# A pre-LN graph layer on one core: SyncE's row fetches on a semaphore per batch, sixteen batches of them, and four edits at the start and the end

## The chip, the cores and the metric

The kernel runs on one core of a Trainium2 chip. The metric is the device time of one execution in microseconds (us), the median of several runs. A core has five engines that run their own instruction streams in order: PE (TensorE, matmuls), DVE (VectorE), ACT (ScalarE), POOL (GpSimd) and SP (SyncE, which issues transfers). SP, ACT and POOL start DMA transfers; engines wait for each other and for transfers through semaphores.

## What is computed

12500 nodes have 160 features each, 64 scalars and 32 vectors of three. 400000 edges, sorted by destination, carry 16 numbers (inputs of a small network that gives 192 weights an edge) and 4 numbers (one scalar and one vector). Cut to what matters:

```python
h  = relu(layernorm(x))                          # per node
y0 = h[:, :64] @ W_l1_0 * attr / 8               # scalars
y1 = einsum('nuc,uv->nvc', h1, W_l1_1) * attr    # vectors
w  = silu(e16 @ W1) @ W2                         # 192 weights per edge
ys0, ys1 = y0[src], y1[src]                      # gather by source
mid = products of w, ys and the edge's 4 numbers # 96 scalars, 96 vectors
z  = zeros.at[dst].add(mid)                      # scatter by destination
o  = z @ W_l2 * attr
out = x + C_S * (h @ W_sc) * attr + C_X * o
```

## The kernel before

**Node stage.** Nodes come in 98 tiles of 128, two tiles to a step. A step does the layernorm and the ReLU on VectorE, turns the rows and maps them by `W_l1` on PE (`map_rows`, L499 in the trace), scales them on ACT and stores them from SP to `y_d` in DRAM. Meanwhile POOL fetches raw rows of `x` for 18 "x batches" (`x_fetch`, L392: 72 indirect DMAs of 128 rows) into `xr`, a buffer of 18 slots. Each fetch issued in step q waits for the maps of step q - 6.

**Main loop.** An edge tile is 128 edges; a batch is four tiles; there are 782 batches, the last with one tile. For each batch the loop does:

- `weigh`: the small network's second matmul on PE (L689) and a copy by ACT (L568);
- `products`: on VectorE a one-hot of the edge's place in its window (`own`, L704), its product with the edge's 4 numbers (`sel`, L706), and the gathered rows times the weights (`pr`, L573 and L577);
- `sums`: on PE the matmul of `sel` and `pr` (L720), which adds the edges of a window into PSUM; a finished window is transposed by VectorE (L726, L727);
- once a group of windows is full: `linear` (L733 on PE, a copy on ACT L735, `place` on VectorE L737), `add` (L745) and `accumulate` into `acc` (L756);
- `extras`: the small network's first layer (L668, L673) for batches to come, a step of the skip path (`skip_load` of `xs` on SP L766, `skip_center` on VectorE L773, turns on PE L780, maps, `skip_add`) and of the x batches, which are mapped inside the loop and need no row of `y_d`.

The order of instructions on every engine is the order of the program text; it is written out by hand. `products(b + 1)` comes ahead of `sums(b)`, and small actions that are put off (`waiting`, two at most) run right behind the products.

**Where the rows come from.** The products need 512 rows of `y_d`, one per edge. Most batches get them by four indirect DMAs on POOL (`gather`, L615), issued six batches ahead and kept in step with the sums. The x batches need none. For some other batches the rows are fetched singly, by a job: a job is (s, b, m), it starts at batch s, fetches 512 rows of 640 bytes spread over m batches, and its rows are used by batch b = s + m + 7. SP has the jobs s = RS, RS + RB, ...; with RB = 58 and RS = 30 these are 12. ACT has 10, with AB = 66 and AS = 102. `row_index` loads the node numbers of eight jobs at a time and `row_place` makes byte places of them; then

- SP does a chunk of 32 rows (`RN`) each m/16 batches: a load of 32 places into registers (L626, the trace's TENSOR_LOAD), then 32 times a register move and a DMA of one row (L638);
- ACT does eight rows (`RU`) in every batch of its job, with a register load for each 16.

The rows of a job go to a slot of `xr` that is free by then. SP's rows are tracked by the framework: it puts each DMA on one of eight semaphores in rotation ("lanes"), a DMA waits until the one before it on its lane has landed, and VectorE's products wait for the lanes. ACT's rows have a semaphore of their own for the batch (`came[b]`); each adds 16, no lane is used, and VectorE waits once for 16 x 512 (`all_rows`).

SP's queue in the loop holds, beside the chunks, the loads of edge data (`xe` L407, 4-number features and indices L415 to L419), a store of `drel` (L433) and the 160 KB loads of `xs` (L766).

**The end.** In the last three batches nothing is put off any more; behind the loop the last two groups get their `linear`, `add` and `accumulate`. Eight tiles of `out` are stored by SP and ACT (L355) after that; a branch for edges outside their windows is not taken with this data. The program's end (L1159) drains every engine.

Of the kernel before, what the change touches and what calls it, by code (L numbers as in the profile page):

```python
# [12 lines left out]
U8 = mybir.dt.uint8  # L13
# [9 lines left out]
D = M0 + 3 * M1  # L23
# [20 lines left out]
LATE = 8  # L44
XB = 18
SK = 9
RB = 58
RS = 30
AB = 66
AS = 102  # L50
RN = 32
AN = 16
RU = 8
# [7 lines left out]
def kernel(  # L61
# [328 lines left out]
    def x_fetch(f, after):  # L390
        u, k = divmod(f, GT)
        fetch = nc.gpsimd.indirect_dma_start(  # L392
            out=xr[:, u, slot(k), :], out_offset=None, in_=x,
            in_offset=bass.IndirectOffsetOnAxis(ap=xi[:, u, k:k + 1], axis=0))
        if after is not None:
            tc.add_manual_dep(fetch.ins, after,
                              mybir.DependencyInfo(mybir.DependencyClass.Sync, mybir.DependencyReason.DATA),
                              reason="rows keep step with the maps")
# [40 lines left out]
    with (  # L439
# [90 lines left out]
        for q in range(len(steps) + 7):  # L530
            if q <= last and steps[q][2] == 0 and more:
                load_x(*more.pop(0))
            for f in range(XB * GT * q // (last + 6), min(XB * GT * (q + 1) // (last + 6), XB * GT)):
                x_fetch(f, mapped.get(q - 6))
            if q == 8:
                e4_load(0)
            for load in loads[2 * q - 24:2 * q - 22] if q >= 12 else []:
                load()
            if q == 24:
                for b in range(min(EARLY, NB)):  # L540
                    features(b)
            if q == 16:
                rows_of_windows()
                lowest(0)
            if q == 18:
                pt = nd_ph.tile([MW, P], F32, name="ph")[:windows_in(0), :]
                turn_low(0, pt)
                most(0, pt)
            if q == 22:
                spread(0, nd_ph.tile([P, MW], F32, name="ph")[:, :windows_in(0)])  # L550
            for stage, lag in ((scales, 3), (leave, 7), (out_of_psum, 4), (roots, 2), (turn_rows, 3), (map_rows, 5),
                               (moments, 0), (center, 1)):
                if 0 <= q - lag <= last:
                    stage(q - lag)
            if q == 2:
                node_weights()
            if q == last + 3:
                nc.vector.tensor_scalar(nm, mv[:, :, 0], -1.0, None, ALU.mult)
                x_split()
                edge_weights()  # L560
                relate(rp, 0)
# [18 lines left out]
    with (  # L580
# [43 lines left out]
        def row_places(j, n, m, engine):  # L624
            q, o = divmod(n, P // RP * GT)
            _, places = nc.values_load_multi_w_load_instructions(  # L626
                ri[RP * j + q:RP * j + q + 1, o:o + m], engines=[engine], min_val=0, max_val=(N - 1) * D * 4,
                skip_runtime_bounds_check_because="places of nodes, as the indices of the other fetches")
            return places

        def row_fetch(j, n, eng, places):
            b = jobs[j][1]
            if n == 0:
                rows[b] = xr[:, slot_of[j], :, :]
            fetches = []
            for m, v in enumerate(places):
                e, k = divmod(n + m, GT)
                fetches.append(eng.dma_start(rows[b].bitcast(U8)[e:e + 1, k, :], y_b[ds(v, D * 4)].unsqueeze(0)))  # L638
            return fetches

        def row_fetch_by_sp(j, n):
            row_fetch(j, RN * n, nc.sync, row_places(j, RN * n, RN, mybir.EngineType.SP))

        def row_fetch_by_act(j, n):
            o = RU * n % AN
            if n == 0:
                came[jobs[j][1]] = tc.alloc_semaphore(f"rows_{j}"), f"rows_{j}"
            sem, group = came[jobs[j][1]]
            for fetch in row_fetch(j, RU * n, nc.scalar, places_of[j][o:o + RU]):
                fetch.then_inc(sem, 16)  # L650
                tc.no_tile_sem_insts.add(fetch.ins.name)
                tc.add_to_no_dep_group(group, fetch.ins)

        def act_places(j, n):
            if RU * n % AN == 0:
                places_of[j] = row_places(j, RU * n, AN, mybir.EngineType.Activation)

        def all_rows(b):
            if b in came:
# [37 lines left out]
        def products(b):  # L697

            n, wt, yg = slots_of(b), wts.pop(b), rows.pop(b)
            all_rows(b)  # L700
            own = selp.tile([P, GT, WN], F32, name="own")
            sel = sels[b] = selp.tile([P, GT, 4, WN], F32, name="sel")[:, :n, :, :]
            pr = prs[b] = prod.tile([P, GT, PC], F32, name="pr")
            nc.vector.tensor_tensor(own[:, :n, :], iota[:, 0:WN].unsqueeze(1).to_broadcast([P, n, WN]),  # L704
                                    wt[:, :n, NW + 4:NW + 5].to_broadcast([P, n, WN]), ALU.is_equal)
            nc.vector.tensor_tensor(sel, own[:, :n, :].unsqueeze(2).to_broadcast([P, n, 4, WN]),  # L706
                                    wt[:, :n, NW:NW + 4].unsqueeze(3).to_broadcast([P, n, 4, WN]), ALU.mult)
            multiply(pr, wt, yg, n)
# [20 lines left out]
        def linear(g):  # L729
            m, za = WN * windows_of(g), zT.pop(g)  # L730
            po = p_x.tile([P, D], F32, name="px")
            for k in range(ZK):
                nc.tensor.matmul(po[:m, :], za[:, k, :m], wo[:, k, :], start=k == 0, stop=k == ZK - 1)  # L733
            os = post.tile([P, D], F32, name="os")
            nc.scalar.activation(os[:m, :], po[:m, :], AF.Copy)  # L735
            place = post.tile([P, 2, P], F32, name="place")
            nc.vector.tensor_scalar(place.rearrange("p h n -> p (h n)"), iota, at[:, g:g + 1], None, ALU.is_equal)  # L737
            o_sb[g] = os, place
# [208 lines left out]
            weigh(1)  # L947
        products(0)
        early = [x for x in groups if x[0] < LOW]
        assert early[-1][0] + early[-1][1] == LOW and first_of[GE] + K + len(early) <= NB  # L950
        for b in range(NB):
            g = group_of[b]
            k = b - first_of[g]
            if b + EARLY < NB:
                features(b + EARLY)
            q, r = divmod(b, KB)
            if b % 8 == 0 and RG * b // 8 < len(jobs):
                row_index(b // 8)
            if r == 0:
                e4_load(q + 1)  # L960
            if r == KB - 4:
                e4_join(q + 1)
            u, v = divmod(b, PER)
            su, sv = skip_of(b)
            if b + 2 < NB:
                weigh(b + 2)
            if units and units[0][0] <= b:
                act_places(*units[0][1:])
            if b + 1 < NB:
                products(b + 1)  # L970
            while waiting and b + K < NB:
                waiting.pop(0)()
            if b % 8 == 2 and RG * (b // 8) < len(jobs):
                row_place(b // 8)
            if v == SB and u < XB:
                x_scale(u)
            if v == 11 and u + 1 < XB:
                hot(u + 1)
            if r == KB - 15 and q + 1 < NQ:
                lowest(q + 1)  # L980
            if r == KB - 8 and q + 1 < NQ:
                relate(rp, q + 1)
                if q + 2 == NQ:
                    most_far()
            if early and b > first_of[GE] + K - 1:
                store(*early.pop(0), nc.sync)
            sums(b)
            for m, part in ((b + AHEAD - 1, slice(2, GT)), (b + AHEAD, slice(0, 2))):
                if AHEAD <= m < NB and m not in xs_of and m not in rows_of:
                    gather(m, part)  # L990
            while chunks and chunks[0][0] <= b:
                row_fetch_by_sp(*chunks.pop(0)[1:])
            while waiting and b + K >= NB:
                waiting.pop(0)()
            extras(b)
            if units and units[0][0] <= b:
                row_fetch_by_act(*units.pop(0)[1:])
        while waiting:
            waiting.pop(0)()
        assert max(b for b in range(NB) if 0 <= skip_of(b)[0] < NU) <= first_of[GE] + K and NQ > 1  # L1000
        for h in ([NG - 2] if NG > 1 else []) + [NG - 1]:
            for k, stage in enumerate((linear, add, accumulate)):
                if h == NG - 1 or min(k, 1) > NB - 1 - first_of[NG - 1]:
                    stage(h)
        order.close()


# [155 lines left out]
```

## Time and profile before

| | before |
|---|---|
| runs | 4938.69, 4900.01, 4903.42 us |
| median | 4903.42 us |
| profiled execution, its own time | 4914.76 us |
| its span | 4912.9 us |
| granted TensorE clock, mean | 0.883 |
| row fetches by SP (L638) | 6144 |
| row fetches by ACT (L638) | 5120 |
| gathers by POOL (L615) | 2965 |
| fetches of x's rows by POOL (L392) | 72 |

The profile is of one execution; its times count from the start of its span. In a row of a group stand line, engine, operation, output<-inputs and count, then busy time and the mean duration in ns, then the idle time ahead of it and what ended most of it. In a row of a source line stand queue, operation, count, the shortest, median and longest duration in ns, and the first and last start in us. In a row of the waits: who, for what, us in total, times, the longest. In a row of a timeline: start, duration, engine, line, operation and how many in a row were put together. In a row of windows: the window, its length, VectorE's busy time there with the count of instructions, granted clock, share of the DMA engines that were busy, GB/s. An engine's name with a q at its end is its sequencer, which issues DMAs.

### The profile page before, as it was taken

Reading aid. Unit: us, or ns where it says so; the run is one execution under the profiler, and the core shown is the slowest. Engines: PE = TensorE matmul, PEld = TensorE weight load, DVE = VectorE, ACT = ScalarE, POOL = GpSimd, SP = SyncE. Lnnn points to the kernel's source line nnn. Section 1 sums busy time; section 2 is a strip of 40 time slices with the busy share of each in tenths; the row PEclk is TensorE's granted clock in tenths of the full one; section 3 lists DMA queues with packets and bytes.
Section 4 is the critical chain, followed back from the end, with each engine's and each line's share of the span. In section 5 each row is a group of like instructions: output and inputs, shape, how many; then the busy total and the mean of one; then the engine's idle time right before and its main releaser. Section 6 shows DMA issues by size and latency. Waiting matters only on the chain. (4 is left out here: it accounts for less than half of the span.)

```text
span 4912.9 us, 76368 instructions
## 1 busy us (share of the span) xinstructions
PE 3930.2 (80%) x17274; PEld 2517.5 (51%) x17274; DVE 2747.3 (56%) x6901; ACT 609.6 (12%) x1863; POOL 2878.2 (59%) x3045
## 2 busy tenths in 40 slices
PE   7778887767778686887777787888887888888888
PEld 7444544444445454554454555555554555555555
DVE  5455555544555454555455565566565666666666
ACT  5011011101101010111011111111111111111110
POOL 6666665646656565555556556566556555565654
PEclk8889898878989898988899898899898888999889
DMA  7222222222222222222222222222222222222223
GB/s 194 67 69 64 70 66 64 60 55 65 65 57 65 58 66 59 64 61 61 56 64 65 63 57 66 61 67 64 64 60 64 61 65 61 65 63 62 65 61 109
DMA packets 272510, 330.52 MB, mean 67 GB/s; under 512 B 84288, under 2 KB 223456, under 8 KB 272048
## 3 DMA queue, kind: packets, MB, share of 16 engines
q0 software_dynamic: 145776, 248.99, 20.5%
q1 hardware_dynamic: 115408, 73.03, 5.3%
q10 hardware_dynamic: 10864, 3.57, 0.4%
q8 instruction: 140, 2.29, 0.2%
q14 instruction: 322, 2.64, 0.2%
HBM read 307.72 MB, written 17.61 MB: 66 GB/s over the span
## 5 line engine op out<-in xcount | busy, mean ns | idle before, releaser
L615 POOL DMA_INDIRECT yg<-y_d,src_q x2965 | 2808.5, 947 | 1962.4 <-issue 702.5
L720 PE MATMUL pz<-pr,sel 128*128 128x320 f32 x6250 | 2122.9, 486 | 51.4 <-issue 23.2
L720 PEld LDWEIGHTS pz<-pr,sel 128*128 128x128 f32 x6250 | 1244.4, 210 | 726.2 <-issue 384.3
L689 PE MATMUL pw<-w,hT 64*128 64x192 f32 x6250 | 825.4, 387 | 331.4 <-DVE pr L577 168.3
L689 PEld LDWEIGHTS pw<-w,hT 64*128 64x128 f32 x6250 | 567.4, 210 | 632.0 <-issue 512.1
L726 DVE STREAM_TRANSPOSE za<-pz 128x160 f32<-128x160 f32 x598 | 206.2, 345 | 1050.5 <-PE pz L720 443.5
L577 DVE TENSOR_TENSOR pr<-pw,yg 128x384 f32<-128x384 f32 x1484 | 749.4, 546 | 0.0
L706 DVE TENSOR_TENSOR sel<-own,pw 128x512 f32<-128x512 f32 x782 | 536.8, 686 | 28.3 <-DVE own L704 1.4
L573 DVE TENSOR_TENSOR pr<-pw,yg 128x512 f32<-128x512 f32 x742 | 506.2, 682 | 9.3 <-DMA yg<-y_d,src_q 9.3
L704 DVE TENSOR_TENSOR own<-iota,pw 128x128 f32<-128x128 f32 x782 | 204.8, 262 | 511.2 <-issue 265.3
L668 PE MATMUL px<-xe,w 32*128 32x512 f32 x782 | 442.1, 648 | 40.5 <-issue 15.9
L568 ACT ACTIVATE pw<-ev 128x20 f32<-128x20 f32 x782 | 149.2, 191 | 2472.6 <-DMA xr<-y_d 526.1
L673 ACT ACTIVATE hT<-px 128x512 f32<-128x512 f32 x391 | 233.2, 597 | 972.4 <-remote 220.5
L733 PEld LDWEIGHTS px<-wo,za 128*128 128x128 f32 x1500 | 227.4, 203 | 153.2 <-issue 77.6
L733 PE MATMUL px<-wo,za 128*128 128x160 f32 x1500 | 261.5, 325 | 53.0 <-issue 11.9
L668 PEld LDWEIGHTS px<-xe,w 32*128 32x128 f32 x782 | 115.6, 185 | 220.0 <-issue 180.4
L745 PE MATMUL px<-os,place 128*128 128x160 f32 x600 | 127.7, 340 | 116.6 <-ACT os L735 94.6
L727 DVE STREAM_TRANSPOSE za<-pz 32x160 f32<-32x160 f32 x598 | 202.0, 338 | 21.6 <-DVE za L726 1.2
L780 PE MATMUL px<-ident,sh 128*128 128x128 f32 x98 | 31.7, 341 | 219.7 <-DVE sh L773 180.3
L745 PEld LDWEIGHTS px<-os,place 128*128 128x128 f32 x600 | 100.0, 209 | 163.2 <-ACT os L735 114.5
L773 DVE TENSOR_SCALAR sh<-xs,mv 128x160 f32<-128x160 f32 x98 | 26.5, 309 | 251.9 <-DMA xs<-in_x 251.9
L780 PEld LDWEIGHTS px<-ident,sh 128*128 128x128 f32 x98 | 15.9, 163 | 241.0 <-issue 176.4
(129 smaller groups left out, 1623.7 us busy)
## 6 DMA issues: line engine op xcount, KB each, us to landing
xr<-y_d SPq DMA_DIRECT2D x6144, 0.6 KB
xr<-y_d ACTq DMA_DIRECT2D x5120, 0.6 KB
yg<-y_d,src_q POOLq DMA_INDIRECT x2965
xe<-in_e SPq DMA_DIRECT2D x196, 128.0 KB
xs<-in_x SPq DMA_DIRECT2D x48, 160.0 KB
acc<-in_x SPq DMA_DIRECT2D x11, 640.0 KB
y_d<-ys SPq DMA_DIRECT2D x11, 640.0 KB
out<-acc SPq DMA_DIRECT2D x11, 640.0 KB
```

The lines of the kernel that those rows point to most:

```text
L573: nc.vector.tensor_mul(pr[:, :n, :].rearrange("p t (x u) -> p t x u", x=2)[:, :, :, 0:M0], wt[:, :n, 0:NW].rearrange("p t (x u) -> p t x u ...
L577: nc.vector.tensor_mul(pr[:, :n, D * x + M0:D * (x + 1)].rearrange("p t (c u) -> p t c u", c=3), wt[:, :n, 96 * x + M0:96 * (x + 1)].unsqu ...
L615: fetch = nc.gpsimd.indirect_dma_start(out=yg[:, slot(t), :], out_offset=None, in_=y_d, in_offset=bass.IndirectOffsetOnAxis(ap=ev4[t // BL ...
L668: nc.tensor.matmul(ph, w1[r, :], xe[r, :], start=True, stop=True)
L673: nc.scalar.activation(hT, ph, AF.Silu, scale=1.0 / math.sqrt(FC_IN))
L689: nc.tensor.matmul(pw[:, k, 0:NW], hT[r, o:o + P], w2[r, :], start=True, stop=True)
L704: nc.vector.tensor_tensor(own[:, :n, :], iota[:, 0:WN].unsqueeze(1).to_broadcast([P, n, WN]), wt[:, :n, NW + 4:NW + 5].to_broadcast([P, n, ...
L706: nc.vector.tensor_tensor(sel, own[:, :n, :].unsqueeze(2).to_broadcast([P, n, 4, WN]), wt[:, :n, NW:NW + 4].unsqueeze(3).to_broadcast([P, ...
L720: mm = nc.tensor.matmul(pz[:, 0:PC], sel[:, slot(t), :, :], pr[:, slot(t), :], start=o == 0, stop=last)
L726: nc.vector.transpose(zT[g][:, :, at_w], pz[:, D:PC].rearrange("p (k u) -> p k u", k=ZK))
L733: nc.tensor.matmul(po[:m, :], za[:, k, :m], wo[:, k, :], start=k == 0, stop=k == ZK - 1)
L745: nc.tensor.matmul(ps[:, h, :], place[:m, h, :], os[:m, :], start=True, stop=True)
```

## The change

1. SP's row fetches get a semaphore for each batch, as ACT's have: `row_fetch` does for both what `row_fetch_by_act` did, so VectorE waits once for an SP batch too.
2. The jobs change: SP 16 of 44 batches from batch 26 (for 12 of 58 from 30), ACT 10 of 65 from 108 (for 10 of 66 from 102).
3. `x_fetch` in step q waits for the maps of step q - 9 and not q - 6.
4. In the last three batches (`ends`): in batch 779 `products(780)` comes behind `sums(779)`, and what waits goes ahead; in batch 780 `linear` of the last group but one comes ahead of `sums(780)`, its `add` behind it. No `extras` are called there, and behind the loop only the last group is left.
5. POOL drains at batch 775, behind its last gather.

```diff
--- before.py
+++ after.py
@@ -44,10 +44,10 @@
 LATE = 8
 XB = 18
 SK = 9
-RB = 58
-RS = 30
-AB = 66
-AS = 102
+RB = 44
+RS = 26
+AB = 65
+AS = 108
 RN = 32
 AN = 16
 RU = 8
@@ -531,7 +531,7 @@
             if q <= last and steps[q][2] == 0 and more:
                 load_x(*more.pop(0))
             for f in range(XB * GT * q // (last + 6), min(XB * GT * (q + 1) // (last + 6), XB * GT)):
-                x_fetch(f, mapped.get(q - 6))
+                x_fetch(f, mapped.get(q - 9))
             if q == 8:
                 e4_load(0)
             for load in loads[2 * q - 24:2 * q - 22] if q >= 12 else []:
@@ -632,28 +632,25 @@
             b = jobs[j][1]
             if n == 0:
                 rows[b] = xr[:, slot_of[j], :, :]
-            fetches = []
+                came[b] = tc.alloc_semaphore(f"rows_{j}"), f"rows_{j}"
+            sem, group = came[b]
             for m, v in enumerate(places):
                 e, k = divmod(n + m, GT)
-                fetches.append(eng.dma_start(rows[b].bitcast(U8)[e:e + 1, k, :], y_b[ds(v, D * 4)].unsqueeze(0)))
-            return fetches
-
-        def row_fetch_by_sp(j, n):
-            row_fetch(j, RN * n, nc.sync, row_places(j, RN * n, RN, mybir.EngineType.SP))
-
-        def row_fetch_by_act(j, n):
-            o = RU * n % AN
-            if n == 0:
-                came[jobs[j][1]] = tc.alloc_semaphore(f"rows_{j}"), f"rows_{j}"
-            sem, group = came[jobs[j][1]]
-            for fetch in row_fetch(j, RU * n, nc.scalar, places_of[j][o:o + RU]):
+                fetch = eng.dma_start(rows[b].bitcast(U8)[e:e + 1, k, :], y_b[ds(v, D * 4)].unsqueeze(0))
                 fetch.then_inc(sem, 16)
                 tc.no_tile_sem_insts.add(fetch.ins.name)
                 tc.add_to_no_dep_group(group, fetch.ins)
 
+        def row_fetch_by_sp(j, n):
+            row_fetch(j, RN * n, nc.sync, row_places(j, RN * n, RN, mybir.EngineType.SP))
+
         def act_places(j, n):
             if RU * n % AN == 0:
                 places_of[j] = row_places(j, RU * n, AN, mybir.EngineType.Activation)
+
+        def row_fetch_by_act(j, n):
+            o = RU * n % AN
+            row_fetch(j, RU * n, nc.scalar, places_of[j][o:o + RU])
 
         def all_rows(b):
             if b in came:
@@ -947,6 +944,7 @@
             weigh(1)
         products(0)
         early = [x for x in groups if x[0] < LOW]
+        assert NG > 1 and NB - first_of[NG - 1] == 2 and NB > K
         assert early[-1][0] + early[-1][1] == LOW and first_of[GE] + K + len(early) <= NB
         for b in range(NB):
             g = group_of[b]
@@ -966,10 +964,13 @@
                 weigh(b + 2)
             if units and units[0][0] <= b:
                 act_places(*units[0][1:])
-            if b + 1 < NB:
+            ends = b + K >= NB
+            if b + 1 < NB and not (ends and b + 2 < NB):
                 products(b + 1)
-            while waiting and b + K < NB:
+            while waiting and (not ends or b + 2 < NB):
                 waiting.pop(0)()
+            if b + 2 == NB:
+                linear(NG - 2)
             if b % 8 == 2 and RG * (b // 8) < len(jobs):
                 row_place(b // 8)
             if v == SB and u < XB:
@@ -990,18 +991,24 @@
                     gather(m, part)
             while chunks and chunks[0][0] <= b:
                 row_fetch_by_sp(*chunks.pop(0)[1:])
-            while waiting and b + K >= NB:
+            if ends and b + 2 < NB:
+                products(b + 1)
+            if b + 2 == NB:
+                add(NG - 2)
+                waiting.append(lambda: accumulate(NG - 2))
+            while waiting and ends:
                 waiting.pop(0)()
-            extras(b)
+            if not ends:
+                extras(b)
+            if b + 1 + AHEAD == NB:
+                nc.gpsimd.drain()
             if units and units[0][0] <= b:
                 row_fetch_by_act(*units.pop(0)[1:])
         while waiting:
             waiting.pop(0)()
         assert max(b for b in range(NB) if 0 <= skip_of(b)[0] < NU) <= first_of[GE] + K and NQ > 1
-        for h in ([NG - 2] if NG > 1 else []) + [NG - 1]:
-            for k, stage in enumerate((linear, add, accumulate)):
-                if h == NG - 1 or min(k, 1) > NB - 1 - first_of[NG - 1]:
-                    stage(h)
+        for stage in (linear, add, accumulate):
+            stage(NG - 1)
         order.close()
 
 
```

## The prediction

> **What bounds the kernel now.** I read the page first: the span, the busy shares and the costliest groups.
>
> ```profile
> span 4912.9 us, 76368 instructions
> ...
> PE 3930.2 (80%) x17274; PEld 2517.5 (51%) x17274; DVE 2747.3 (56%) x6901; ACT 609.6 (12%) x1863; POOL 2878.2 (59%) x3045
> ...
> L615 POOL DMA_INDIRECT yg<-y_d,src_q x2965 | 2808.5, 947 | 1962.4 <-issue 702.5
> ...
> L773 DVE TENSOR_SCALAR sh<-xs,mv 128x160 f32<-128x160 f32 x98 | 26.5, 309 | 251.9 <-DMA xs<-in_x 251.9
> ```
>
> No engine is full: PE is busy for 80% of the span, POOL, which issues the gathers, for 59%. The last row is the odd one. The 98 centerings of the skip path work for 26.5 us and stand idle for 251.9 us, all of it until `xs` has come, and `xs` is one of 48 plain loads from SP's queue. So I went to the waits.
>
> ```profile
> POOL yg L615 <- issue: 702.5, 2276, 1.1
> POOL yg L615 <- PE pz L720: 662.6, 283, 27.3
> ...
> DVE sh L773 <- DMA xs<-in_x: 251.9, 18, 29.8
> ```
>
> Eighteen stalls, up to 29.8 us long: VectorE stops for a load that SP issues too late. POOL in its turn waits 662.6 us for PE's sums, so it is held in step and is not alone the bound. What makes SP late is seen in its own lines, the row fetches (L638) and the loads of their addresses into registers (L626), with ACT's beside them:
>
> ```profile
> L638 SPq DMA_DIRECT2D xr<-y_d x6144: 2/225/1398, 257.5 to 4586.0; - x199
> ...
> L638 ACTq DMA_DIRECT2D xr<-y_d x5120: 3/217/1394, 726.1 to 4794.4; - x197
> ```
>
> ```profile
> L626 ACTq TENSOR_LOAD <-ri x320: 4/1216/1442, 724.6 to 4783.4; - x160
> L626 SPq TENSOR_LOAD <-ri x192: 14/2118/2501, 255.2 to 4566.3; - x192
> ```
>
> 6144 rows in 192 chunks of 32 take SP from 255.2 to 4586.0, 4331 us or 22.6 us a chunk. SP does little but this, and its rows do not all go at one rate:
>
> ```profile
> 2015.41 26.89 SPq L638 DMA_DIRECT2D xr<-y_d  x32
> ...
> 2046.57 12.80 SPq L638 DMA_DIRECT2D xr<-y_d  x32
> ```
>
> ```profile
> 3012.38 38.75 SPq L638 DMA_DIRECT2D xr<-y_d  x64
> 3052.79 1.41 SPq L407 DMA_DIRECT2D xe<-in_e  x2
> 3055.04 19.71 SPq L638 DMA_DIRECT2D xr<-y_d  x32
> 3074.85 0.42 SPq L766 DMA_DIRECT2D xs<-in_x  x1
> ```
>
> The group of 64 holds one register load of 2.12 us. Without it, five chunks took 96.0 us, 0.600 us a row; the quickest chunk went at 12.80/32 = 0.40, the slowest at 0.84. At 0.600 a chunk is 19.2 + 2.12 = 21.3 us, and 192 of them are 4093 us. The other 238 us of SP's stage are its loads (`xe`, `xs`, the edge features) and what these wait for. An `xs` load stands behind chunks of this length in an in-order queue: 3074.85 is right behind one.
>
> The pace of the loop says the same. Each batch makes one `own` (L704) and one `sel` (L706), so half the count in these rows is batches:
>
> ```profile
> 400.00:720.00 320.00, 54.10 (x114) 0.89 0.26 66
> 1000.00:2000.00 1000.00, 151.13 (x316) 0.86 0.24 61
> 4600.00:4780.00 180.00, 29.42 (x62) 0.91 0.24 61
> ```
>
> That is 320/57 = 5.61 us a batch in the first part of the stage, 1000/158 = 6.33 in the middle, and 180/31 = 5.81 when SP's rows are over (after 4586) and ACT's still run. The 12 jobs cover 12 x 58 = 696 batches, and 4331/696 = 6.22 us: the loop goes at SP's pace. About 252/696 = 0.36 us of it are the stalls, which leaves 5.86, close to the 5.81.
>
> **The change, part by part.**
>
> *Rows by SP.* 16 jobs of 44 batches take the place of 12 of 58: 8192 rows for 6144, so 2048 more row fetches, 2048 more register moves and 64 more register loads on SP. A chunk of 32 rows then falls due each 44/16 = 2.75 batches and not each 3.625. At 6.22 us a batch that is 17.1 us for what took 22.6. At the old price SP cannot do it, so the price of a row decides this change. The stage covers 16 x 44 = 704 batches; at the old pace that is 4331 x 704/696 = 4381 us, and the 238 us of other loads become 241. SP keeps the old pace at 256 x (32p + 2.12) + 241 = 4381, so **p = 0.439 us a row** is the point of decision.
>
> What the new semaphore does to p the trace shows in two ways. SP's waits on its lanes, which go, are small:
>
> ```profile
> SPq L638 <- DMA xr<-y_d: 81.3, 167, 1.4
> SPq L407 <- PE px L668: 15.3, 2, 15.0
> ```
>
> 81.3 us over 6144 rows are 0.013 us a row, so by the waits p falls to 0.587 only. But ACT fetches rows with the same code, in the same stage, already with a semaphore per batch:
>
> ```profile
> 2657.57 2.64 ACTq L638 DMA_DIRECT2D xr<-y_d  x8
> 2660.42 2.40 ACTq L638 DMA_DIRECT2D xr<-y_d  x8
> 2672.23 2.70 ACTq L638 DMA_DIRECT2D xr<-y_d  x8
> 2675.13 5.44 ACTq L638 DMA_DIRECT2D xr<-y_d  x8
> ```
>
> ```profile
> 3007.70 3.05 ACTq L638 DMA_DIRECT2D xr<-y_d  x8
> 3010.96 5.22 ACTq L638 DMA_DIRECT2D xr<-y_d  x8
> ...
> 3029.98 2.80 ACTq L638 DMA_DIRECT2D xr<-y_d  x8
> ```
>
> Seven groups of eight took 24.25 us: 0.433 us a row. The lower bound of p is 0.40, SP's quickest chunk; the upper is 0.600, no change at all. I take ACT's 0.43: same instruction, same memory, same gathers beside it, and the kind of semaphore is the difference that the code shows. The other difference, eight rows at a time and not 32, is my main doubt. The sum: 256 x (13.76 + 2.12) + 241 = 4306 us against 4381, so **-75 us**.
>
> *Four batches fewer for POOL.* ACT keeps its 10 jobs (65 batches long for 66). SP's four jobs more leave 16 gathers fewer. One costs POOL 1.26 us from start to start (116.18 to 117.44 below), 20 us in all. The loop is held by SP's queue as long as SP is the bound, and POOL waits 662.6 us for sums anyway, so I count nothing beside the 75 us; if POOL were the bound it would be -20.
>
> The Trainium skill speaks against a larger gain: "DMA: Bandwidth & Descriptors", section "Issuing engines are not separate DMA queues", says that transfers begun by different engines run on the same 16 DMA engines, and that spreading them saves only the issuing time. By that rule alone the part would be worth those 20 us. The trace agrees in that SP's rate swings between 0.40 and 0.84 us a row; whether the shared engines are the reason no row here shows.
>
> *Products' waits.* VectorE waits once for an SP batch's semaphore at its full count and no longer on SP's lanes. The wait is queued ahead of `own` and holds all later VectorE work; SP's last chunk of a job falls some eight batches, about 50 us, before its products, which is the cover. SP would have to be 50 us late; if it is, that is the slow rival below. I count 0.
>
> *x's rows wait for maps nine steps back.*
>
> ```profile
> 14.55 0.95 POOL L392 DMA_INDIRECT xr<-in_x,xi  x1 [1.74 <-PE po L499]
> ...
> 112.94 0.97 POOL L392 DMA_INDIRECT xr<-in_x,xi  x1 [0.30 <-issue]
> ...
> 116.18 0.95 POOL L615 DMA_INDIRECT yg<-y_d,src_q  x1 [2.28 <-DMA ri<-in_src]
> 117.44 0.94 POOL L615 DMA_INDIRECT yg<-y_d,src_q  x1 [0.30 <-issue]
> ```
>
> Early fetches wait for PE's maps (1.74 us at 14.55), and an older map frees them sooner. But the last fetch, at 112.94, waits for nothing but issue, and behind it the first gather waits 2.28 us more: for the last rows of `y_d` by the order of the code, though the row names another transfer. What POOL gains goes into that wait. If earlier fetches delay the node loads it can cost as much: -2 to +2, I take 0.
>
> *The tail.*
>
> ```profile
> 4898.86 1.52 PE L733 MATMUL px<-wo,za 128*128 128x160 f32 x10
> ...
> 4900.78 0.81 PE L745 MATMUL px<-os,place 128*128 128x160 f32 x4
> ...
> 4904.60 0.80 DVE L756 SCALAR_TENSOR_TENSOR acc<-px,a_sb,acc 128x160 f32 x2 [1.51 <-PE px L745]
> 4906.30 1.15 SPq L355 DMA_DIRECT2D out<-acc  x2
> ```
>
> ```profile
> L1159 POOLq DRAIN  x3: 45/123/5700, 4906.3 to 4912.6; - x3
> L1159 SPq EVENT_SEMAPHORE  x3: 17/17/28, 4910.4 to 4912.8; - x3
> ```
>
> Today POOL's drain begins at 4906.3 and takes 5.70 us, to 4912.0, while SP has its stores home at 4910.4. With the drain issued six batches before the end, the others' tenth of a microsecond is left: -1.5 us, and 0 if it only moves. For the group turns, the next to last group's linear and add (1.52 + 0.81 us on PE) come ahead of products and sums. If they leave the last chain that is -2.3; if their wait for the transposes holds PE, in order, ahead of the sums it is +2.3. I take 0.
>
> **The sum**: -75 - 1.5 is -76.5 on the profiled execution's own 4914.8 us (its span 4912.9 and 1.9 around it): **4838 us**. That execution stands 11 us above the median of the three runs (4903.4) and inside their spread, so I leave the number as it is: 65 us or 1.3% below the median. A change of about 1% is what this measurement can tell from none.
>
> **Rivals.**
>
> *A. SP's price does not fall, and SP holds the loop back: slower.* For it: lane waits are only 0.013 us a row, and fast and slow chunks stand side by side on the same lanes. Against it: ACT's 0.433. It decides from 0.439 up. At 0.457 the stage is 256 x (14.62 + 2.12) + 241 = 4526, +145, so 5060. At 0.600 it is 5699, +1318; as more time with POOL at rest lets the rows in excess go at 0.40, rather 2048 x 0.40 + 64 x 2.12 = 955 less the 50 us that the stage is longer, so about 5820.
>
> *B. SP stops being the bound.* At 0.40 its stage is 256 x 14.92 + 241 = 4061, under the 704 x 5.81 = 4090 that the rest of the loop needs; the 251.9 us of stalls go: 4663. For it: 5.61 and 5.81 us a batch where SP does not hold the loop. Against it: the price must be that of the quickest chunk all through.
>
> *C. Only the issuing moves.* Sixteen gathers of 1.26 us go, rows stay as slow in the mean, but the loads of `xs` land no later since SP's chunks are due more evenly: 4915 - 20 = 4895, no change. For it: POOL's gathers are the largest issue in the loop, and this is what the cited rule gives. Against it: VectorE's stalls are on SP's loads.
>
> **Chances.** Forecast 0.40 (its own range 4760 to 4870, p from 0.42 to 0.434), A 0.28, B 0.12, C 0.20. Faster by over 1%, below 4854: 0.36 of the forecast's 0.40 and B, 0.48. Within 1%: 0.04 of the forecast, C, and 0.04 of A where p is just over the decision, 0.28. Slower: 0.24. The range goes from 4690 (B with nine tenths of the stalls gone) to 5060 (A at 0.457); it leaves out about half of A and half of B, 0.20.
>
> **What would show it.** Right: SP's stage of about 4300 us with 8192 rows, groups of 32 of about 14 us, the `xs` stalls down from 251.9 to some 180, 6.1 us a batch in the middle, 2949 gathers, a POOL drain near 0.1 us at the end. Wrong: chunks of 17 us and more with `xs` stalls of 400 us and up (A), stalls near 0 (B), or chunks as now and the same pace (C). If ACT's groups of eight rows become slower than 0.433 as SP's become faster, the two share a limit and the price that I took from ACT does not carry over.

## The result, and the profile after

The changed kernel takes **5605.5 us** (5585.6 to 5626.0), the kernel before 4911.0 beside it: a ratio of 1.142, 95% interval 1.138 to 1.147. The forecast was 4838 us with a range to 5060. It went the way of rival A, which had 5820 us for its whole price.

The page of the changed kernel, the rows that answer to those of before:

```profile
span 5607.6 us, 80445 instructions
...
PE 3973.1 (71%) x17274; PEld 2537.4 (45%) x17274; DVE 2750.7 (49%) x6902; ACT 606.9 (11%) x1863; POOL 2868.9 (51%) x3029
...
L615 POOL DMA_INDIRECT yg<-y_d,src_q x2949 | 2799.0, 949 | 2668.6 <-PE pz L717 1431.9
...
L770 DVE TENSOR_SCALAR sh<-xs,mv 128x160 f32<-128x160 f32 x98 | 25.4, 300 | 824.7 <-DMA xs<-in_x 824.7
```

No engine has much more work than before (PE 3973 us for 3930, POOL 2869 for 2878); every share has fallen because the span has grown by 694.7 us. The stalls of VectorE on `xs` grew from 251.9 to 824.7 us, 572.8 of those 694.7. The waits (who, for what, us in total, times, longest) show what follows from that: POOL, held in step with PE's sums, stands 1431.9 us for them, 662.6 before.

```profile
POOL yg L615 <- PE pz L717: 1431.9, 309, 49.3
DVE sh L770 <- DMA xs<-in_x: 824.7, 29, 54.7
PE px L777 <- DVE sh L770: 702.7, 30, 50.6
```

The rows fetched singly (now L639) and SP's register loads, by source line:

```profile
L639 SPq DMA_DIRECT2D xr<-y_d x8192: 2/225/1695, 258.8 to 5343.7; - x200
L639 ACTq DMA_DIRECT2D xr<-y_d x5120: 3/217/895, 816.4 to 5471.0; - x197
```

```profile
L626 SPq TENSOR_LOAD <-ri x256: 15/2106/2560, 256.6 to 5325.2; - x128
```

SP's stage is 5085 us for 704 batches, 7.22 us a batch, where it was 6.22. In windows the loop goes at that pace: 139 batches in the second thousand us, 7.19 each.

```profile
1000.00:2000.00 1000.00, 133.01 (x278) 0.82 0.21 53
```

So it looks as if the kernel is held by SP's queue as before, with a third more rows in it; the experiments test that. SP's stage is 5085 - 4331 = 754 us longer; less some 50 us for the eight batches more that it covers, that is the whole loss.

What a row costs is seen best where POOL stops. SP's timeline around 3040 us, and POOL's:

```profile
2995.92 44.33 SPq L639 DMA_DIRECT2D xr<-y_d  x64
3040.52 0.21 SPq L433 DMA_DIRECT2D drel_d<-drel  x1
3043.01 10.24 SPq L639 DMA_DIRECT2D xr<-y_d  x32
```

```profile
3038.93 0.95 POOL L615 DMA_INDIRECT yg<-y_d,src_q  x1 [0.31 <-issue]
3040.19 0.95 POOL L615 DMA_INDIRECT yg<-y_d,src_q  x1 [0.30 <-issue]
3041.44 0.95 POOL L615 DMA_INDIRECT yg<-y_d,src_q  x1 [0.30 <-issue]
```

While gathers come, 64 rows with one register load take 44.33 us, (44.33 - 2.11)/64 = 0.66 us a row. The last gather ends at 3042.4; from 3043.0 on 32 rows take 10.24 us, 0.32 a row. ACT's groups in the same 40 us of gathers:

```profile
3002.69 2.37 ACTq L639 DMA_DIRECT2D xr<-y_d  x8
3013.37 2.67 ACTq L639 DMA_DIRECT2D xr<-y_d  x8
...
3022.44 3.68 ACTq L639 DMA_DIRECT2D xr<-y_d  x8
```

That is 0.30 to 0.46 us a row, with the same kind of semaphore. SP now has ACT's semaphore and not ACT's price.

One stretch could mislead, so here is the count over whole traces. I count a row from its register move to the next one's, and take gathers with under 0.5 us between them as one train. In the kernel before, 3586 rows inside a train took 0.63 us in the mean, and 1491 rows with no gather beside them 0.38. In the changed kernel 3813 rows inside a train took 0.61, and 3229 without a gather 0.35. The remaining 869 and 894 rows lie partly beside a gather, at 0.85 and 0.82. That the whole core stands still, and not POOL alone, does not explain it: in the changed kernel 739 rows with POOL at rest and PE busy (over 80% of the two us around their start) took 0.33 us, and 491 rows with POOL busy (over 60%) and PE mostly idle (under 30%) took 0.63. This is a coincidence in time, on one chip; no run there leaves the gathers out.

### The profile page after: what moved, and what is told of

The parts are those of the page before. It is cut to its first block, busy times and chain, and to the rows that moved or that the text cites. A ratio compares the mean times of both kernels' runs of the same rounds, so it can differ in the third digit from the quotient of the medians.

```text
span 5607.6 us, 80445 instructions
## 1 busy us (share of the span) xinstructions
PE 3973.1 (71%) x17274; PEld 2537.4 (45%) x17274; DVE 2750.7 (49%) x6902; ACT 606.9 (11%) x1863; POOL 2868.9 (51%) x3029
## 4 chain that ended last, share of the span: by engine, by line
SPq 22%; PE 16%; issue 13%; DVE 2%; another core or an unknown queue 1%; DMA 1%; ACTq 1%; ACT 0%; DVEq 0%; POOL 0%
SPq L639 18%; PE pz L717 8%; PE pw L686 3%; SPq L626 3%; PE px L665 2%; PE px L730 1%; DVE pr L577 1%; PE px L742 1%; ACTq L639 1%; SPq L407 1%; DMA xs<-in_x 1%; DVE pr L573 0%; PE px L824 0%; DVE za L723 0%
## 5 line engine op out<-in xcount | busy, mean ns | idle before, releaser
L615 POOL DMA_INDIRECT yg<-y_d,src_q x2949 | 2799.0, 949 | 2668.6 <-PE pz L717 1431.9
L665 PE MATMUL px<-xe,w 32*128 32x512 f32 x782 | 457.9, 668 | 141.9 <-DMA xe<-in_e 87.2
L770 DVE TENSOR_SCALAR sh<-xs,mv 128x160 f32<-128x160 f32 x98 | 25.4, 300 | 824.7 <-DMA xs<-in_x 824.7
```

What stands on the lines that cost most here:

```text
L615: fetch = nc.gpsimd.indirect_dma_start(out=yg[:, slot(t), :], out_offset=None, in_=y_d, in_offset=bass.IndirectOffsetOnAxis(ap=ev4[t // BL ...
L665: nc.tensor.matmul(ph, w1[r, :], xe[r, :], start=True, stop=True)
```

## The experiments

Two theories stood against each other. **Theory 1**: the jobs are the cost; SP's queue is the bound, a row on it keeps its price, and it got a third more rows. **Theory 2**: the semaphore or one of the small edits (the maps nine steps back, the end) costs. A rival to both: only the place of the `xs` loads behind the rows costs, not SP's rate.

The runs fell on chips of two speeds, and a time can only be compared with the kernel before on the same one. On the chip of the first four runs the kernel before takes 4907.4 us, about as in the profile the prediction was made from; on the three chips of all later runs it takes 3832 to 3833 us. I call them the first and the later chips; the first was one chip at one time, so whether the difference belongs to the chip or to that time is not shown.

**First chip, the old jobs on the changed kernel.**

```diff
-RB = 44
-RS = 26
-AB = 65
-AS = 108
+RB = 58
+RS = 30
+AB = 66
+AS = 102
```

> The changed kernel with the old jobs (SP 12 of 58 from 30, ACT 10 of 66 from 102): the semaphore per batch, the nine steps and the edits of the tail alone. Theory 1 (the jobs are the cost: a row on SP keeps its price, SP's queue has 31% more to do): within 1% of before, 4850 to 4950 us, SP's stage 4250 to 4400 us, VectorE's stalls on xs about 250 us. Theory 2 (the semaphore or one of the small edits is the cost): 5200 us or more.

4906.6 us, ratio 1.001 (0.998 to 1.003). The semaphore, the nine steps and the edits of the tail together are worth nothing that can be measured, and cost nothing. Theory 2 falls.

**First chip, the new jobs on the kernel before**: the same four lines the other way round, on the old lanes.

> The kernel before with the new jobs only (SP 16 of 44 from 26, ACT 10 of 65 from 108), rows still on the rotating lanes. Theory 1: 5550 to 5720 us, as slow as the changed kernel or up to 108 us slower (81.3 us of lane waits times 8192/6144). Theory 2: near 4900 us. If the semaphore brings what its makers could want of it, this one is slower than the changed kernel by over 1%.

5621.9 us, ratio 1.145 (1.140 to 1.150); the changed kernel had 1.142 (1.138 to 1.147). SP's stage, by source line:

```profile
L638 SPq DMA_DIRECT2D xr<-y_d x8192: 1/225/1412, 260.1 to 5368.9; - x200
```

5109 us for 5085. The jobs alone make the whole loss, and on this chip the semaphore takes nothing measurable of it away (16 us, and the intervals overlap). The four lines also move ACT's ten jobs, which were not tried by themselves; SP's longer stage accounts for the loss without them.

**First chip, ten jobs for SP** (RB = 72, RS = 27, AB = 66, AS = 102 on the changed kernel).

> The changed kernel with fewer jobs for SP: 10 of 72 from 27 (ACT 10 of 66 from 102), so 5120 rows by SP and 8 gathers more than before. Theory 1: a chunk falls due each 4.5 batches, 26 us at 5.8 us a batch, and takes 21 to 23, so SP is no longer the bound: stalls on xs under 60 us, 4690 to 4780 us. Rival (POOL's gathers are the bound as soon as SP is not): 4900 to 4950 us.

**4766.1 us, ratio 0.971 (0.967 to 0.976)**: faster than both kernels, by taking work off SP and giving it back to POOL. No stall on `xs` is left in its waits. Its SP timeline and its pace:

```profile
3010.39 41.44 SPq L639 DMA_DIRECT2D xr<-y_d  x64
...
3056.00 20.61 SPq L639 DMA_DIRECT2D xr<-y_d  x32
```

```profile
1000.00:2000.00 1000.00, 162.67 (x340) 0.88 0.27 65
```

The rows are as dear as ever, (41.44 - 2.11 + 20.61)/96 = 0.62 us, though SP is no longer behind; so the price does not come from SP being late. But 170 batches fit into 1000 us, 5.88 us each, the 5.86 that the prediction had worked out for a loop without the stalls. What holds the loop at 5.88 us there is not shown.

**First chip, 16 jobs with the `xs` loads issued by ACT.**

```diff
-            node_dma(t, m, lambda rows, k, p: nc.sync.dma_start(xs[:p, k, :], by_tile(x[rows, :])))
+            node_dma(t, m, lambda rows, k, p: nc.scalar.dma_start(xs[:p, k, :], by_tile(x[rows, :])))
```

> The changed kernel with 16 jobs, its xs loads issued by ACT and not by SP. Theory 1 (SP's rate is the limit): the stalls on xs go, but others take their place (late rows, late loads of edge data), and the time stays at SP's pace, 5450 to 5600 us. Rival (only the place of the xs loads behind the rows costs, SP could keep up): 5605 - 825 = 4780 us, at most 4900.

5584.2 us, ratio 1.137 (1.132 to 1.142). The 824.7 us of stalls on `xs` are gone and the time stays. The waits show what has taken their place:

```profile
DVE neg L196 <- DMA dst_q<-in_dst: 506.8, 22, 34.6
DVE own L701 <- DMA xr<-y_d: 398.0, 16, 39.0
PE px L665 <- DMA xe<-in_e: 191.3, 18, 20.8
```

Each is another load of the same queue, and the 16 waits for rows are one for each SP job. The rival falls: it is SP's rate, and whatever SP delivers last is what the loop waits for.

**Later chips, the two kernels again.** The kernel before and the changed one, without an edit.

> The kernel before, unchanged, to have its trace on the chip of this call, since two chips so far took 4907 and 3832 us for it. Where it takes about 3830 us: groups of 32 rows on SP in 10 to 11 us (0.33 us a row), stalls on xs under 10 us, POOL's gathers without pauses. Where it takes about 4900 us: as in the first profile, 0.58 us a row and over 200 us of stalls on xs.

> The changed kernel, unchanged, on the chip of this call. Where the kernel before takes 3830 us a row on SP costs 0.33 us, so 256 x (10.6 + 2.12) + 241 = 3497 us for 704 batches, 4.97 us a batch, and the loop otherwise goes at 3560/782 = 4.6: SP is the bound there too, stalls on xs of 200 us and up, 3880 to 3950 us, slower by 1 to 3%. Rival (16 jobs fit where rows are quick; four batches of gathers fewer are a gain of 20 us): 3800 to 3830 us. Where the kernel before takes 4900 us: 5550 to 5650 us.

The kernel before took 3831.4 us, the changed one **3939.5 us, ratio 1.028 (1.027 to 1.030)**. The gathers on the page of the kernel before, SP's lines, and its pace:

```profile
L615 POOL DMA_INDIRECT yg<-y_d,src_q x2965 | 2809.1, 947 | 904.2 <-issue 631.9
```

```profile
L638 SPq MOVE xr<-y_d x6144: 29/29/42, 217.7 to 3535.3; - x199
L638 SPq DMA_DIRECT2D xr<-y_d x6144: 224/228/381, 217.8 to 3535.4; - x199
```

```profile
1000.00:2000.00 1000.00, 200.79 (x426) 0.97 0.33 81
```

And of the changed kernel on such a chip, by source line, waits and window:

```profile
L639 SPq DMA_DIRECT2D xr<-y_d x8192: 224/228/453, 217.2 to 3713.2; - x200
```

```profile
DVE sh L770 <- DMA xs<-in_x: 230.0, 22, 24.8
```

```profile
1000.00:2000.00 1000.00, 192.47 (x406) 0.94 0.33 78
```

There POOL's idle time is mostly the 0.3 us between gathers (904.2 us for 1962.4), and rows are quick beside them all the same: no row's DMA on SP takes over 0.46 us in these two traces, where the changed kernel had up to 1.70 on the first chip. The DMA engines are busier there, 0.33 of the second thousand us for 0.24 on the first chip, both in the kernel before, so their load by itself does not make a row dear. The stage was forecast at 3497 us with 0.33 us a row and is 3496. Even so 16 jobs are too many: SP needs 4.97 us a batch, and the loop goes at 1000/213 = 4.69 with 12 jobs, where SP does not hold it.

**Later chips, the new jobs on the lanes.**

> The kernel before with the new jobs (16 of 44, ACT 10 of 65), rows on the rotating lanes. Where the kernel before takes 3830 us, SP is the bound with 16 jobs: 3935 to 4060 us, that is as slow as the changed kernel there (3939.5) or slower by up to 118 us, the 88.2 us of lane waits in the trace of before times 8192/6144. If it is slower by 30 us and more, the semaphore is worth that where SP is the bound. Where the kernel before takes 4900 us: 5600 to 5640 us as it was.

4118.8 us, ratio 1.074 (1.072 to 1.076), 179 us more than with the semaphore on such a chip, a larger difference than I had bounded it by. SP's lane waits and its stage:

```profile
SPq L638 <- DMA xr<-y_d: 131.4, 331, 1.6
```

```profile
L638 SPq DMA_DIRECT2D xr<-y_d x8192: 224/228/497, 218.2 to 3897.5; - x200
```

The stage is 3679 us for 3496: 183/8192 = 0.022 us a row. So where SP is the bound and its rows are quick, the semaphore per batch is worth 4% of the time (this kernel also lacks the small edits; with the old jobs, below, they are worth nothing measurable on such a chip); the profile's waits name 131 of the 183 us.

**Later chips, other numbers of jobs**: 8 (RB = 88, RS = 24), 11 (RB = 64, RS = 24) and 14 (RB = 50, RS = 24), with ACT's 10 of 66 from 102, and the old 12.

> The changed kernel with 8 jobs of 88 batches from 24 for SP (ACT 10 of 66 from 102), 8 gathers more than with ten jobs. Theory 1: SP was not the bound with ten, so fewer rows on SP gain nothing, and the gathers (8 x 1.26 us) cost: 4766 to 4800 us. Rival (each row on SP slows the rest of the core, by the transfers it adds): under 4740 us.

> The changed kernel with 11 jobs of 64 from 24 for SP (ACT 10 of 66 from 102). Theory 1: a chunk falls due each 4 batches, 23.4 us at 5.86 us a batch, and takes 21 to 23 with SP's other loads, just at the limit: stalls on xs come back in part, 4740 to 4830 us, within 1.5% of ten jobs. If POOL were the bound, four gathers fewer than with ten jobs would make it 5 us faster and not more.

> The changed kernel with 14 jobs of 50 from 24 for SP, ACT 10 of 66 from 102. Where the kernel before takes 3830 us: SP needs 224 x (10.6 + 2.12) + 239 = 3088 us for 700 batches, 4.41 us a batch against the loop's 4.6: just not the bound; 3815 to 3850 us. Where it takes 4900 us: SP's work is between that of 12 and 16 jobs, 5150 to 5350 us.

> The changed kernel with the old jobs (12 of 58, ACT 10 of 66): semaphore, nine steps and the edits of the tail alone. Where the kernel before takes 3830 us: SP is not the bound, its 88 us of lane waits are hidden, the tail is worth 1 to 3 us; 3825 to 3835 us, ratio 0.998 to 1.001. Where it takes 4900 us: 4890 to 4920 us as it was.

| SP's jobs | us | ratio to before, 95% interval |
|---|---|---|
| 8 | 3852.2 | 1.005 (1.003 to 1.007) |
| 11 | 3837.7 | 1.001 (1.000 to 1.002) |
| 12 | 3832.3 | 1.000 (0.999 to 1.001) |
| 14 | 3824.7 | 0.998 (0.997 to 0.999) |
| 16 | 3939.5 | 1.028 (1.027 to 1.030) |

From 8 to 14 jobs each is worth (3852.2 - 3824.7)/6 = 4.6 us, near the 4 x 1.26 = 5.0 us that its four gathers cost POOL; then SP becomes the bound, and two more jobs cost 115 us. The Trainium skill, "DMA: Bandwidth & Descriptors", section "Issuing engines are not separate DMA queues", has it that spreading transfers over engines saves the issuing time only; these rows agree, up to the point at which the engine that is given the work has no time left. The expectations for 8 and 11 jobs were written for the first chip, and their absolute times could not come out. Of the one for eleven jobs the first half, stalls on `xs` again, did not come here (its waits have none); the second half, four gathers fewer make 5 us, is what the differences show. The old 12 jobs, with the semaphore and all small edits, are again not to be told from the kernel before. Fourteen jobs beat the kernel before by 0.2% on such a chip and the changed one by 2.9%; on the first chip they were not run.

**SP's chunks of 8 rows, ten jobs of 72.**

```diff
-RN = 32
+RN = 8
```

> Ten jobs of 72 again, but SP's chunks are of 8 rows and not of 32, as ACT's are (four times as many register loads, 640). Account a (32 rows on end make a row dear, and ACT's are cheap because there are eight): groups of eight at 0.40 to 0.45 us a row; 640 x (8 x 0.43 + 2.12) = 3558 us of SP, under the 4219 us of the stage; 4740 to 4790 us as with chunks of 32. Account b (the price belongs to SP's queue beside the gathers, whatever the length): 0.57 to 0.60 us a row; 640 x (8 x 0.58 + 2.12) = 4326 us and the other loads, SP is the bound again; 4850 to 5000 us.

> Ten jobs of 72, SP's chunks of 8 rows, on the chip of this call. Where the kernel before takes 4900 us: 0.40 to 0.45 us a row and 4740 to 4790 us if 32 rows on end make a row dear, 0.57 to 0.60 us a row and 4850 to 5000 us if the price is that of SP's queue beside the gathers. Where it takes 3830 us: 3842 us as it was.

> Ten jobs of 72, SP's chunks of 8 rows. Where the kernel before takes 4900 us: 0.40 to 0.45 us a row and 4740 to 4790 us if 32 rows on end make a row dear; 0.57 to 0.60 us a row and 4850 to 5000 us if the price is that of SP's queue beside the gathers. Where it takes 3830 us: 3842 us as it was.

All three fell on later chips: 3842.4, 3842.5 and 3842.6 us, ratios 1.003 (1.002 to 1.004). A group of 32 rows there holds three register loads of 8 places each (the group from the second of the three runs, the loads from the first):

```profile
2000.46 12.83 SPq L639 DMA_DIRECT2D xr<-y_d  x32
```

```profile
L626 SPq TENSOR_LOAD <-ri x640: 686/794/1158, 213.0 to 3652.3; - x160
```

(12.83 - 3 x 0.79)/32 = 0.33 us a row, as with chunks of 32. That does not tell a from b on the first chip.

**No gathers, 16 jobs.** The gathers behind the first six batches are left out, and later batches take those six batches' rows, so the output is another.

```diff
-        halves, came, places_of = {}, {}, {}
+        halves, came, places_of, kept = {}, {}, {}, {}
...
+            if b >= AHEAD:
+                rows[b] = kept[b % AHEAD]
+                return
             if part.start == 0:
-                rows[b] = ygp.tile([P, GT, D], F32, name="yg")
+                rows[b] = kept[b] = ygp.tile([P, GT, D], F32, name="yg")
```

> The changed kernel with 16 jobs, with POOL's gathers left out behind the first six batches (later batches take the rows of these again, so the output is another). Theory (the gathers beside them make SP's rows dear): 0.32 to 0.36 us a row, a chunk of 32 in 10 to 12 us; SP's stage 256 x (10.9 + 2.12) + 241 = 3574 us, 4000 us in all, less if PE and VectorE allow. Rival (SP's row has its price of its own, whatever POOL does): 0.57 us a row or more, SP's stage over 5000 us and the time as with the gathers, 5450 to 5600 us.

> The changed kernel with 16 jobs, POOL's gathers left out behind the first six batches, on the chip of this call. If the gathers make SP's rows dear where the kernel before takes 4900 us, then without them this runs there as on the other chip, 3850 to 3950 us with rows at 0.33 us. Rival (that chip's SP is slow by itself): rows at 0.58 us and 5400 us or more. Where the kernel before takes 3830 us it is 3900 us as it was.

> The changed kernel with 16 jobs, POOL's gathers left out behind the first six batches. Where the kernel before takes 4900 us: 3850 to 3950 us with rows at 0.33 us if the gathers make SP's rows dear; 5400 us or more with rows at 0.58 us if SP is slow by itself there. Where the kernel before takes 3830 us: 3900 us as it was.

> The changed kernel with 16 jobs, POOL's gathers left out behind the first six batches. Where the kernel before takes 4900 us: 3850 to 3950 us with rows at 0.33 us if the gathers make SP's rows dear; 5400 us or more with rows at 0.58 us if SP is slow by itself there. Where the kernel before takes 3830 us: 3900 us as it was.

3900.1, 3901.3, 3895.7 and 3899.3 us, one execution each, all on later chips; the question for the first chip is not answered by it. It answers another one. SP's timeline and the wait on `xs`:

```profile
2000.18 15.49 SPq L642 DMA_DIRECT2D xr<-y_d  x41
...
2019.54 23.25 SPq L642 DMA_DIRECT2D xr<-y_d  x64
```

```profile
DVE sh L773 <- DMA xs<-in_x: 348.5, 27, 31.2
```

Without a single gather in the loop, 16 jobs are still slower than the kernel before with its 2965 gathers. SP sets that pace: (23.25 - 2.11)/64 = 0.33 us a row, and the stage, from 198.3 to 3676.8, is 3478 us where it was 3496 with the gathers.

## Why the prediction was wrong, point by point

**What bounds the kernel: right.** SP's queue, its stage of 22.6 us a chunk, and the `xs` stalls as its sign. Ten jobs took the stalls away and the loop went at 5.88 us a batch.

**The point of decision: right as a formula.** With 0.439 us a row from rows of before, the forecast turned on one price. With the stage as it was measured it gives 4914.8 + 5085 - 4381 = 5619 us, and the profiled execution took 5609. Eight thousand rows make 0.01 us of it 82 us, and a range of 370 us was four and a half hundredths wide: too narrow for a price between 0.40 and 0.600.

**The price of a row: the step that failed.** It read "I take ACT's 0.43", since "the kind of semaphore is the difference that the code shows". Measured by the same formula the price is (5085 - 256 x 2.11 - 241)/8192 = 0.525 us. It fell from 0.600, and not by the semaphore: on the lanes it is (5109 - 256 x 2.11 - 241)/8192 = 0.528. What fits the fall in the traces is that POOL now stands longer (2668.6 us idle for 1962.4): rows without a gather beside them are 41% of those counted, 25% before. The new mix at the old prices alone would take 0.600 to 0.554; the rest is not explained. The trace of before had the right size in it, 0.013 us a row of lane waits, and I set it below a likeness to another engine whose groups differ in engine and in length too. The "quickest chunk" of 0.40 was only the quickest of the five chunks shown. The same trace has seven chunks under 12 us, and the quickest, 0.32 us a row, runs for most of its time beside a standing POOL:

```profile
2710.68 10.34 SPq L638 DMA_DIRECT2D xr<-y_d  x32
```

```profile
2717.81 0.94 POOL L615 DMA_INDIRECT yg<-y_d,src_q  x1 [16.14 <-PE pz L720]
```

On the later chips the semaphore is worth 0.022 us a row, of the size of those lane waits and not of ACT's advantage.

**Rival A: right in kind.** Its 5820 us gave the rows in excess 0.40 us. At the 0.32 of the one chunk of 10.24 us above, 2048 x 0.32 + 64 x 2.11 = 790, less the 50, gives 5655, 50 us from the measured time; by the stages the rows in excess cost (8192 x 0.525 - 6144 x 0.600)/2048 = 0.30. It had 0.28.

**B and C.** B's mechanism is real, but it takes fewer jobs and not cheaper rows: ten jobs, 4766 us. C fails on the first chip; its 20 us for 16 gathers are what the later chips show between 8 and 12 jobs (3852.2 - 3832.3).

**The small edits.** Counted at 0 and -1.5 us. Rows of the end and of the start in the changed kernel:

```profile
L1004 POOLq DRAIN  x1: 7532/7532/7532, 5575.6 to 5575.6; - x1
```

```profile
L1166 POOLq DRAIN  x3: 39/41/146, 5602.1 to 5607.3; - x3
L1166 SPq EVENT_SEMAPHORE  x3: 17/17/28, 5606.4 to 5607.5; - x3
```

```profile
110.07 0.96 POOL L392 DMA_INDIRECT xr<-in_x,xi  x1 [0.30 <-issue]
118.98 0.95 POOL L615 DMA_INDIRECT yg<-y_d,src_q  x1 [7.96 <-DMA ri<-in_src]
```

POOL's first drain of the end, at 5602.1, is 0.04 us for 5.70. The wait has moved and is not gone: the added drain at batch 775 (L1004) takes 7.53 us, beside the loop's last batches. From the first store to the end there are 5607.6 - 5602.0 = 5.6 us where there were 4912.9 - 4906.3 = 6.6: -1.0 us. The last of x's rows is fetched at 110.07 for 112.94, and the first gather still waits, to 118.98 for 116.18: POOL gains nothing, as counted, and the first gather is 2.8 us later in this execution. The turns of the last groups were not tried by themselves. With the old jobs, all of it and the semaphore together measure 1.001 (0.998 to 1.003) on the first chip and 1.000 (0.999 to 1.001) on a later one.

## What to carry to other kernels

An in-order queue whose own work fills its stage can be the bound, though no engine's busy share shows it; ask what it needs per turn of the loop before giving it more. A cost per item that decides the sign is to be taken from that queue's own rows, in the stretches that differ only by what is to be changed, and not from a neighbour that is cheaper for reasons unknown. And where chips differ in which of two queues is the scarce one, the best split between them differs too: ten jobs cost 0.3% on the later chips (in chunks of 8) and gain 2.9% on the first.

## What the runs showed of the hardware

The same kernel took 4907 us (4891 to 4925) on one chip and 3832 (3829 to 3841) on others, 1.28 times as long. The gathers themselves cost the same, 947 ns each. What differs is seen best in the lines of SP: in the kernel before a register move has a median of 29 ns on both, but takes at most 42 on a later chip and up to 1407 on the first. Its mean row of 0.600 us on the first chip is 0.13 in the move, 0.22 in the DMA's issue and 0.25 in pauses between instructions; on a later chip the 0.351 us are 0.03, 0.23 and 0.09. So the move and the pauses are dearer, and not the DMA's issue in the mean. Over the whole trace of the changed kernel a row on SP costs 0.61 us inside a train of gathers and 0.35 without on the first chip; on a later one 0.33 with and without. PE is slower too: its granted clock in the second thousand us is 0.86 on the first chip and 0.97 on a later one, and a matmul of the sums (L720) takes 486 ns for 457; VectorE's busy time is the same, 2747 us for 2755. Why the chips differ stays open, and so does why ACT's rows were cheaper than SP's beside the same gathers on the first: the coincidence with the gathers is seen in its traces, but the runs that would have shown it, without gathers and with SP in groups of eight, did not fall on it.
